# Idle ticks behind the last gather, matmuls with unread results at the start, and no marker copies in the last stage of a two-layer graph kernel

## The chip, the cores and the metric

The kernel runs on one core of a Trainium2 chip. A core has five engines that run side by side, each through its own list of instructions in order: TensorE (PE) multiplies matrices, VectorE (DVE) and GpSimd (POOL) do elementwise work and reductions, ScalarE (ACT) evaluates functions, and SyncE (SP) issues most of the transfers between the chip's memory and the core. GpSimd issues the indirect transfers, gathers and scatters by row number. Engines wait for each other through semaphores. The metric is the device time of one execution, in microseconds (us), as the median of several runs.

## The reference

There are 16 graphs of 1024 nodes with 128 features. Layer 0 is masked attention; layer 1 thins out each graph's edges and runs three graph convolutions with batch norms between them.

```python
h = max(layernorm(x), 0)
q, k, v = (relu(h @ W.T + b) for W, b in ((Wq, bq), (Wk, bk), (Wv, bv)))
att = softmax(where(adj, q @ k.T, -9e15))
x = x + relu((att @ v) @ Wo.T + bo)

h = max(layernorm(x), 0)
adj_d = dilate(adj)        # node after node: a node with more than 10 edges drops some of them
def sage(h, k):            # rows scaled to length 1
    out = (adj_d @ h / deg) @ Wr[k] + h @ Wx[k] + b[k]
    return out / norm(out)
h1 = bn(relu(sage(h, 1)));  h2 = bn(relu(sage(h1, 2)));  h3 = bn(relu(sage(h2, 3)))
x = x + concat(h1, h2, h3) @ Wl + bl
```

The batch norm takes mean and variance over all 16 graphs and all nodes, so no graph can enter a round before every graph has left the one before.

## The kernel before, in words

All of `fast` is one program written out by hand. Generators issue a few instructions and then yield; a loop decides which generator goes on when. Each engine then has its instructions in the order in which they were issued, and nothing is reordered later. `Clock` holds work that is put off: `later(n, fn)` (called `put_off` inside `Dilation`) runs `fn` in the n-th `tick()` from now.

**Start.** `load_x(0)` loads the features of graph 0, `load_adj(0)` (that is, `Dilation.load`) loads its adjacency matrix in eight blocks of 128 rows. Each block gets two instructions that run over 128x1024 elements: an exponential on ScalarE that writes the 0/1 matrix as bf16 and sums it (line 167), and a count of its zeros, which for graphs 0 and 1 is on VectorE (line 174). The buffer `st` of a block has three copies, so that a load waits for the exponential and the count of three blocks earlier. `project(0)` then makes layer norm on VectorE (`moments`, lines 564 to 583, and `normalize`, line 588), eight transposes on TensorE (line 598) and the projections to q, k and v (line 676). Two blocks of the matrix are processed ahead of `project(0)`, and 15 pieces of it are issued with one clock tick after each.

**Attention.** Sixteen steps of 48 ticks each, in which TensorE alternates between scores (line 697) and values (line 713), with the work of the dilation threaded between them by tables of ticks. For each pair of graphs the dilation sorts nodes, and `gather` (13 pieces) builds a one-hot matrix, turns it into row numbers (line 296), fetches 128 rows of the adjacency matrix by an indirect transfer on GpSimd (line 301), runs a scan over them on VectorE (line 305), makes codes (line 308), transposes them on TensorE (line 312), copies the result on ScalarE (line 316) and multiplies again (line 320). `solve` then iterates over a group of graphs. The gather of the last graph, 15, is not finished when attention ends: the plan puts its 13 pieces at ticks 68 to 94 of step 15, and only ticks up to 69 are run, so 11 pieces are left.

**Round one** of the convolutions (loop at line 1085) handles one graph per eight ticks. `mix` issues its matmuls and squares and norms, `turn` its transposes, `normalize` on GpSimd the layer norm of graphs further ahead. After each tick `beside1` (line 1073) advances `rest`, which is first what is left of the last gather and then `solve` for graphs 12 to 15 (118 pieces). How many pieces per tick is set by `PIECES1 / TICKS1`, 131 pieces in 120 ticks. Every fourth tick also moves the store of graph 15's layer 0 result, eight row scatters on GpSimd.

**Rounds two and three** are similar without the dilation. In round three the rows go back to their original order: graphs other than the five of `STAY` are scattered to a buffer `y_d` and loaded back, graphs of `STAY` are scattered straight to the output in the last stage. `pace_scatters` (line 1143) hands out one scatter in two of three ticks; ahead of each it issues on GpSimd a copy of one column into a tile `mark` that nothing reads (line 1149), out of the tile that VectorE wrote last, so that GpSimd waits for VectorE there.

**The last stage** (loop at line 1265) multiplies by the last third of `Wl` on TensorE (lines 1231 and 1239), adds on VectorE (line 1024), stores eleven graphs by SyncE (line 1247) and scatters the five of `STAY`, eight scatters of 128 rows each, on GpSimd (line 540). Then a flag is read, all engines meet at a barrier, and a general version would run if the flag said so.

Of the kernel before, what the change touches and what calls it, by code (L numbers as in the profile page):

```python
# [7 lines left out]
F32 = mybir.dt.float32  # L8
# [72 lines left out]
class Dilation:  # L81
# [76 lines left out]
    def load(self, b):  # L158

        nc = self.nc  # L160
        ab = self.rows.tile([P, NB, N], BF, name="ab", bufs=AB)
        diag = bass.AP(tensor=ab.tensor, offset=ab.offset, ap=[list(ab.ap[0]), [N + P, NB], [1, P]])
        self.A[b] = ab, diag
        for k in range(NB):
            st = self.rows.tile([P, N], F32, name="st", bufs=ST)
            nc.sync.dma_start(st, self.adj[b, k * P:(k + 1) * P, :])
            nc.scalar.activation(ab[:, k, :], st, AF.Exp, bias=self.one_k, scale=ONE_K,  # L167
                                 accum_out=self.deg[:, b, k:k + 1])
            yield
            junk = self.rows.tile([P, N], BF, name="junk", bufs=1)  # L170
            zeros = self.zeros[:, b, k:k + 1]
            if b < 2:

                nc.vector.scalar_tensor_tensor(junk, st, 0.0, self.onesf[:, 0:1].to_broadcast([P, N]),
                                               op0=OP.is_equal, op1=OP.mult, accum_out=zeros)
            else:
                nc.scalar.activation(junk, st, AF.Exp, scale=-ZERO_K, accum_out=zeros)  # L177
            yield

    def mirror(self, b, k):  # L180
# [332 lines left out]
def fast(ctx: ExitStack, tc: tile.TileContext, a, out, vp):  # L513
# [94 lines left out]
    def pieces(name, rows, pool):  # L608

        n = len(rows)  # L610
        v = pool.tile([3, 2, P], F32, name="pcv", bufs=1)[:, :n]
        part = pool.tile([3, 2, P], BF, name="pcp", bufs=1)[:, :n]
        acc = pool.tile([3, 2, P], F32, name="pca", bufs=1)[:, :n]
        res = pool.tile([3, n, 4, P], BF, name=name, bufs=1)
        for i, (base, more) in enumerate(rows):
            if base is None:
                nc.vector.tensor_copy(v[:, i, :], more)
            elif more is None:
                nc.vector.tensor_copy(v[:, i, :], base)
            else:  # L620
                nc.vector.tensor_add(v[:, i, :], base, more)
        for i in range(3):
            nc.vector.tensor_copy(part, v)
            if i == 0:
                nc.vector.tensor_scalar(acc, part, identf[:3, i:i + 1], None, op0=OP.mult)
            else:
                nc.vector.scalar_tensor_tensor(acc, part, identf[:3, i:i + 1], acc, op0=OP.mult, op1=OP.add)
            if i < 2:
                nc.vector.tensor_sub(v, v, part)
        nc.vector.tensor_copy(res, acc[:, :, None, :].to_broadcast([3, n, 4, P]))  # L630
        return [res[:, i].rearrange("p a b -> p (a b)") for i in range(n)]
# [9 lines left out]
    with ExitStack() as s1:  # L641
# [7 lines left out]
        def load_x(b):  # L649
            X[b] = xpool.tile([P, NB, XW], F32, name="xt")  # L650
            nc.sync.dma_start(X[b][:, :, :D], x_in[b].rearrange("(k p) d -> p k d", p=P))
            nc.vector.tensor_copy(X[b][:, :, D].bitcast(I32), dil.node32)

        def project(b):


            xt = X[b]
            hn = att.tile([P, NB, D], F32, name="hn", bufs=1)
            hT = att.tile([P, N], F32, name="hT", bufs=1)
            at = dict(name="pm", bufs=1) if b else dict(name="ps", bufs=2)  # L660
            ln = att.tile([P, 2, NB // 2, 2], F32, name="ln")
            engine = nc.gpsimd if b else nc.vector
            yield from moments(xt, att, ln[:, 0], ln[:, 1], engine)
            yield from normalize(engine, hn, xt, ln[:, 0], ln[:, 1])
            yield from transposed(hn, hT, lambda: aps, at["name"], at["bufs"])
            Q[b] = att.tile([P, N], F32, name="qT")
            K[b] = att.tile([P, N], F32, name="kT")
            vT = att.tile([P, N], F32, name="hn", bufs=1)
            V[b] = att.tile([P, NB, D + 1], F32, name="vw")
            nc.vector.memset(V[b][:, :, D], 1.0)  # L670
            for w, bias, o in ((wq, bq, Q[b]), (wk, bk, K[b]), (wv, bv, vT)):
                if o is vT:
                    at = dict(name="pm", bufs=1)
                for g in range(2):
                    pp = aps.tile([P, 512], F32, **at)
                    nc.tensor.matmul(pp, w, hT[:, 512 * g:512 * g + 512], start=True, stop=True)
                    later(1, lambda g=g, pp=pp, bias=bias, o=o: nc.scalar.activation(
                        o[:, 512 * g:512 * g + 512], pp, AF.Relu, bias=bias))
                    yield
            for g in range(2):  # L680
                pp = aps.tile([P, 4, P], F32, **at)
                for k in range(4):
                    j = 4 * g + k
                    nc.tensor.matmul(pp[:, k, :], vT[:, j * P:(j + 1) * P], wo, start=True, stop=True)
                later(1, lambda g=g, pp=pp: nc.vector.tensor_add(V[b][:, 4 * g:4 * g + 4, :D], pp,
                                                                 bo[:, None, :].to_broadcast([P, 4, P])))
                yield
# [67 lines left out]
        def solve_pieces(b0, b1):  # L755
            return 9 * ITER + 3 + 13 * (b1 - b0)
# [42 lines left out]
        bq, bk, bv = (column("L0_gnn_b" + n) for n in "qkv")  # L799
        bo = row_all("L0_gnn_bo")  # L800
        load_x(1)
        values0 = project(0)
        for _ in range(5 + 4 + 2 + 4):
            next(values0)
# [87 lines left out]
                    H[b] = enter(b)  # L892
                _advance(H[b][1])
        clock.flush()
        assert all(gen is gathering[B - 1] for gen, ticks in agenda if ticks)
        dil.tail = True
    load_x2(2)

    def last_of_dilation():

        yield from gathering[B - 1]
        yield from dil.solve(LAST, B)

    def last_stores():
# [158 lines left out]
    with tc.tile_pool(name="ps1", bufs=2, space=PSUM, reuse_waits="tile") as ps:  # L1063
        for _ in H[0][1]:
            clock.tick()
        rest, stores = last_of_dilation(), last_stores()
        checks = dil.verdict(a["nodemask"], vp, recips)
        _advance(checks)

        tick, TICKS1, PIECES1 = 0, 8 * (B - 1), 13 + solve_pieces(LAST, B)  # L1070
        entering = iter(())

        def beside1():
            nonlocal tick
            tick += 1
            _advance(rest, tick * PIECES1 // TICKS1 - (tick - 1) * PIECES1 // TICKS1)
            if tick % 4 == 0:
                _advance(stores)

            if tick in range(8 * LAST + 1, 8 * LAST + 15, 2) or tick > TICKS1:  # L1080
                _advance(checks)
            _advance(entering, tick * ENTER // 8 - (tick - 1) * ENTER // 8)

        prev = None
        for b in range(B):
            if b == B - 1:
                drain(rest)
            if b + 2 < B:
                H[b + 2] = enter(b + 2)
                entering = H[b + 2][1]  # L1090
            if b + 3 < B:
                load_x2(b + 3)
            ob = work.tile([P, NB, P], F32, name="ob")
            parts = {"mix": mix(b, H.pop(b)[0], wx[0], wr[0], bias0, None, ob, on_scalar=True)}
            if prev:
                parts["turn"] = turn(*prev)
            if b + 1 < B:
                parts["next"] = H[b + 1][1]
            in_turn(["mix", "mix", "next", "mix", "turn", "next", "mix", "turn"], parts, beside1)
            entering = iter(())  # L1100
            prev = (b, ob, r1[b // 2][:, b % 2, :])
        clock.flush()
        drain(turn(*prev))
        clock.flush()
        drain(checks)
# [5 lines left out]
    with big:  # L1111
# [26 lines left out]
        rows_r = lambda b: blocks(r2[b // 2][:, b % 2, :])  # L1138
        rows_z = lambda b: blocks(r1[b // 2][:, b % 2, :])
        mark = few.tile([P, 1], F32, name="mark")  # L1140
        waiting, ticks3 = [], 0

        def pace_scatters():


            nonlocal ticks3
            ticks3 += 1
            if ticks3 % 3 and waiting and waiting[0][0] <= ticks3:
                nc.gpsimd.tensor_copy(mark, last[0])  # L1149
                waiting.pop(0)[1]()  # L1150

        with tc.tile_pool(name="w3", bufs=3, reuse_waits="tile") as own:
# [109 lines left out]
        clock.flush()  # L1262
        (wl2,), pr = batchnorm(2, [wl[:, 2, :]])
        bias, = pieces("pc3", [(zrow, pr[:, 0, :])], few)
        for i, b in enumerate(order):
            parts = {"final": final(b, hs[b]), "raised": raise_next(i + 1)}
            in_turn(["raised", "final", "raised", "final"], parts, pace_scatters)
# [588 lines left out]
```

## Time and profile before

| | us |
|---|---|
| median of 3 runs | 1238.69 (1237.64 to 1240.6) |
| the profiled execution | 1234.29 |
| its span | 1232.4 |
| TensorE busy | 1095.0 (89%) |
| VectorE busy | 881.5 (72%) |
| ScalarE busy | 726.6 (59%) |
| GpSimd busy | 573.6 (47%) |

Stages in the span, by the first matmuls of each: attention from 14.4 us, round one from 787 us, round two from about 924 us, the last stage from about 1161 us. Times in what follows are microseconds from the start of the span. In a timeline line the first number is the start, the second the busy time of the merged group, then engine, line, operation, tiles (written, then read) and count; in brackets stands how long the engine sat idle before it, and what released it. In a line of waits stand the waiting instruction, what it waited for, the sum of waiting, the number of waits and the longest. A 128x512 matmul in f32 appears as two matrix passes.

### The profile page before, as it was taken

The page shows a single profiled execution, that of the slowest core. Times are in us where ns is not written, and L with a number is a line of the kernel's source. Part 1 is how long each engine was busy: PE and PEld are TensorE (multiplying, and loading weights), DVE is VectorE, ACT ScalarE, POOL GpSimd, SP SyncE. Part 2 cuts the span into 40 slices and gives each one's busy share as a digit, 9 for nine tenths or more (in the row PEclk, how much of TensorE's full clock was granted, in tenths as well). Part 3 has the DMA queues.
Part 4 walks back from the last instruction along what each step waited for, and adds up shares of the span by engine and source line. Part 5 has one row for each costly group of instructions (what it writes and reads, how often), then busy time and mean ns, then how long its engine had stood idle before and what let it go on. Part 6 is the DMA issues. An engine that isn't in the chain of part 4 may idle for free. (4 is left out here: it accounts for less than half of the span.)

```text
span 1232.4 us, 22348 instructions
## 1 busy us (share of the span) xinstructions
PE 1095.0 (89%) x7775; PEld 820.4 (67%) x7775; DVE 881.5 (72%) x2630; ACT 726.6 (59%) x1570; POOL 573.6 (47%) x1082
## 2 busy tenths in 40 slices
PE   4899999999899899899899888588769979999894
PEld 2467677666576676566567656477658758988773
DVE  5767567579788578678778778589877876666642
ACT  5578788777677777678677652266554542333320
POOL 0330752651742742743644524769400004777686
PEclk9899999999999999999999999789889989999897
DMA  6544244344244344244334411415000013778564
GB/s 197 157 132 139 92 139 152 99 130 150 87 137 144 98 137 153 86 126 151 97 127 122 125 31 39 122 42 135 1 1 1 1 35 109 228 218 239 167 185 126
DMA packets 118147, 143.45 MB, mean 116 GB/s; under 512 B 9212, under 2 KB 94088, under 8 KB 118024
## 3 DMA queue, kind: packets, MB, share of 16 engines
q1 hardware_dynamic: 106120, 110.78, 30.3%
q0 software_dynamic: 11904, 31.15, 7.7%
q8 instruction: 63, 1.03, 0.4%
q14 instruction: 60, 0.49, 0.1%
HBM read 113.39 MB, written 28.51 MB: 115 GB/s over the span
## 5 line engine op out<-in xcount | busy, mean ns | idle before, releaser
L713 PEld LDWEIGHTS po<-vw,e 128*128 128x128 f32 x2048 | 273.1, 195 | 65.7 <-issue 65.3
L713 PE MATMUL po<-vw,e 128*128 128x129 f32 x2048 | 306.9, 284 | 0.0
L697 PE MATMUL ps<-qT,kT 128*128 128x512 f32 x512 | 272.0, 615 | 0.8 <-ACT e L699 0.8
L700 DVE TENSOR_TENSOR e<-e,ab 128x512 f32<-128x512 f32 x256 | 177.9, 696 | 110.4 <-ACT e L699 108.8
L699 ACT ACTIVATE e<-ps 128x512 f32<-128x512 f32 x256 | 153.0, 598 | 107.1 <-PE ps L697 84.4
L540 POOL DMA_INDIRECT x_d<-xt,slot x128 | 142.6, 1114 | 38.8 <-issue 34.9
L167 ACT ACTIVATE ab<-st,d_one_k 128x1024 bf16<-128x1024 f32 x128 | 146.9, 1148 | 0.3 <-DMA st<-in_adj_dram 0.3
L576 POOL TENSOR_SCALAR ln_t<-ln_st 128x8 f32<-128x8 f32 x31 | 8.0, 258 | 288.5 <-DVE ln_st L569 230.0
L177 ACT ACTIVATE junk<-st 128x1024 bf16<-128x1024 f32 x112 | 118.3, 1056 | 0.0
L540 POOL DMA_INDIRECT y_d<-y,nodes x88 | 86.2, 979 | 29.1 <-issue 28.6
L722 ACT ACTIVATE o<-po,recips 128x128 f32<-128x128 f32 x128 | 46.7, 367 | 72.1 <-DVE recips L720 72.0
L697 PEld LDWEIGHTS ps<-qT,kT 128*128 128x128 f32 x512 | 79.0, 194 | 7.6 <-issue 3.1
L1019 ACT ACTIVATE r<-pt 128x512 f32<-128x512 f32 x74 | 44.5, 601 | 58.7 <-PE pt L1007 58.7
L588 POOL TENSOR_SCALAR hn<-xt,ln 128x128 f32<-128x128 f32 x120 | 75.9, 644 | 1.6
L965 ACT ACTIVATE sq<-po 128x512 f32<-128x512 f32 x80 | 47.7, 596 | 47.1 <-PE po L956 44.1
L951 PE MATMUL po<-ws,r 128*128 128x128 f32 x512 | 74.8, 292 | 0.0
L305 DVE TENSOR_TENSOR_SCAN left<-rows 128x1024 f16<-128x1024 f32 x16 | 38.2, 2389 | 50.1 <-DMA rows<-in_adj_dram,row 50.1
L1016 DVE BATCH_NORM_STATS2 stats<-r 128x6 f32<-128x512 f32 x74 | 50.9, 689 | 29.4 <-ACT r L1019 28.9
L951 PEld LDWEIGHTS po<-ws,r 128*128 128x128 f32 x512 | 64.9, 199 | 8.6 <-issue 6.8
L968 DVE TENSOR_REDUCE nrm<-sq 128x4 f32<-128x512 f32 x80 | 53.9, 676 | 22.8 <-ACT sq L965 21.4
L1149 POOL COPY mark<-y 128x1 f32<-128x1 f32 x30 | 5.7, 191 | 135.7 <-DVE y L1024 132.8
L588 POOL TENSOR_SCALAR hn<-xt 128x128 f32<-128x128 f32 x112 | 55.9, 510 | 27.0 <-PE pt L598 26.2
(300 smaller groups left out, 2426.8 us busy)
## 6 DMA issues: line engine op xcount, KB each, us to landing
st<-in_adj_dram SPq DMA_DIRECT2D x128, 512.0 KB, 3.7
r<-y_d SPq DMA_DIRECT2D x22, 512.0 KB, 5.2
xt<-x_d SPq DMA_DIRECT2D x16, 524.0 KB, 3.8
xt<-in_x_dram SPq DMA_DIRECT2D x16, 512.0 KB, 4.2
x<-x_d SPq DMA_DIRECT2D x16, 512.0 KB, 4.4
out_dram<-r SPq DMA_DIRECT2D x11, 512.0 KB, 3.4
x_d<-xt,slot POOLq DMA_INDIRECT x128, 2.8
y_d<-y,nodes POOLq DMA_INDIRECT x88, 3.5
```

Of the source, the lines that this page charges most:

```text
L167: nc.scalar.activation(ab[:, k, :], st, AF.Exp, bias=self.one_k, scale=ONE_K, accum_out=self.deg[:, b, k:k + 1])
L177: nc.scalar.activation(junk, st, AF.Exp, scale=-ZERO_K, accum_out=zeros)
L540: d = nc.gpsimd.indirect_dma_start(out=dst, out_offset=bass.IndirectOffsetOnAxis(ap=slots, axis=0), in_=src, in_offset=None)
L588: engine.tensor_scalar(hn[:, k, :], xt[:, k, :D], minus[:, k // 2, k % 2, None], rstd[:, k // 2, k % 2, None], op0=OP.add, op1=OP.mult)
L697: nc.tensor.matmul(p, K[b][:, k * P:(k + 1) * P], Q[b][:, c], start=True, stop=True)
L699: later(1, lambda: nc.scalar.activation(e, p, AF.Exp))
L700: later(2, lambda: nc.vector.tensor_mul(e, e, AB_[b][:, k, c]))
L713: nc.tensor.matmul(po[:, q % 2, :], E[k][:, i * P:(i + 1) * P], V[b][:, k, :], start=(k == 0), stop=(k == NB - 1))
L951: nc.tensor.matmul(po[:, i, :], hT[:, c:c + P], wxk, start=(i == 3), stop=False)
L965: later(1, lambda: nc.scalar.activation(sq, halves[g], AF.Square))
L968: nc.vector.tensor_reduce(n[:, 0, 4 * g:4 * g + 4], sq, axis=AX.X, op=OP.add)
L1016: nc.vector.bn_stats(stats[:, 2 * b + g, :], d)
```

## The change

Four edits. In `load`, the zero count becomes a function; for graph 0's first two blocks it is put off by eight ticks, which places both counts behind six of the eight `normalize` instructions of `project(0)`. Ahead of `project(0)` GpSimd fills a 128x512 tile with ones and TensorE multiplies it six times with the identity matrix into a PSUM tile that is next written by the v projection; nothing reads the six results. In round one, after the gather's piece 5 (the indirect transfer) six ticks go by without a piece of `rest`, after piece 7 (the codes) five; `PIECES1` becomes 11 + 11 + 118 = 140 for the same 120 ticks. From the third batch norm on, `pace_scatters` issues no copy into `mark`.

```diff
@@ load
-            junk = self.rows.tile([P, N], BF, name="junk", bufs=1)
+            junk = lambda: self.rows.tile([P, N], BF, name="junk", bufs=1)
             zeros = self.zeros[:, b, k:k + 1]
-            if b < 2:
-
-                nc.vector.scalar_tensor_tensor(junk, st, 0.0, self.onesf[:, 0:1].to_broadcast([P, N]),
+
+            def count(st=st, zeros=zeros):
+                nc.vector.scalar_tensor_tensor(junk(), st, 0.0, self.onesf[:, 0:1].to_broadcast([P, N]),
                                                op0=OP.is_equal, op1=OP.mult, accum_out=zeros)
+
+            if b == 0 and k < 2:
+
+                self.put_off(8, count)
+            elif b < 2:
+
+                count()
             else:
-                nc.scalar.activation(junk, st, AF.Exp, scale=-ZERO_K, accum_out=zeros)
+                nc.scalar.activation(junk(), st, AF.Exp, scale=-ZERO_K, accum_out=zeros)
@@ fast, ahead of project(0)
         load_x(1)
+
+        some = att.tile([P, 4 * P], F32, name="e", bufs=16)
+        nc.gpsimd.memset(some, 1.0)
+        idle = aps.tile([P, 4 * P], F32, name="pm", bufs=1)
+        for _ in range(6):
+            nc.tensor.matmul(idle, identf, some, start=True, stop=True)
         values0 = project(0)
@@ fast, between attention and round one
-        assert all(gen is gathering[B - 1] for gen, ticks in agenda if ticks)
+        (gather_left,) = (len(ticks) for gen, ticks in agenda if ticks)
...
+    GATHER_IDLE = {5: 6, 7: 5}
+
     def last_of_dilation():
 
-        yield from gathering[B - 1]
+        for part in range(13 - gather_left, 13):
+            next(gathering[B - 1])
+            for _ in range(1 + GATHER_IDLE.get(part, 0)):
+                yield
         yield from dil.solve(LAST, B)
@@ round one
-        tick, TICKS1, PIECES1 = 0, 8 * (B - 1), 13 + solve_pieces(LAST, B)
+        tick, TICKS1, PIECES1 = 0, 8 * (B - 1), gather_left + sum(GATHER_IDLE.values()) + solve_pieces(LAST, B)
@@ pace_scatters
-        waiting, ticks3 = [], 0
+        waiting, ticks3, marked = [], 0, True
...
-                nc.gpsimd.tensor_copy(mark, last[0])
+                if marked:
+                    nc.gpsimd.tensor_copy(mark, last[0])
@@ last stage, after the third batch norm
         bias, = pieces("pc3", [(zrow, pr[:, 0, :])], few)
+        marked = False
         for i, b in enumerate(order):
```

On VectorE the new order in round one puts, between the row numbers and the scan of the last gather, the reduction, the maximum, the reciprocal and the two scalings of graph 0 (lines 968, 990, 994, 997). On TensorE it puts all of graph 1's matmuls and the four transposes of each half of graph 0's result (line 1007) ahead of the codes' transposes (line 312). On ScalarE the two copies of line 316 come behind the square root of graph 1 (line 991). GpSimd's order changes only by the new memset and the 40 copies that are gone.

## The prediction

> **What bounds the kernel.** The chain that ended last is short here (only the final scatters), so I read each of the three places where the change acts in the timelines and waits, and the stretches around them in busy time by window. TensorE is busiest (89%), so what counts is where it waits.
>
> Start, timeline of VectorE and TensorE:
>
> ```profile
> 7.03 1.23 DVE L174 SCALAR_TENSOR_TENSOR junk<-st,d_onesf 128x1024 bf16<-128x1024 f32 x1 [3.87 <-DMA st<-in_adj_dram]
> ...
> 9.62 1.40 DVE L569 BATCH_NORM_STATS2 ln_st<-xt 128x6 f32<-128x256 f32 x4
> ...
> 13.97 2.14 DVE L588 TENSOR_SCALAR hn<-xt,ln 128x128 f32<-128x128 f32 x8
> ...
> 16.43 3.65 PE L676 MATMUL ps<-hT,w_L_gnn_Wq 128*128 128x512 f32 x4
> 19.87 2.11 PE L676 MATMUL ps<-hT,w_L_gnn_Wk 128*128 128x512 f32 x4
> ```
>
> VectorE idles 3.87 us for the matrix, counts twice (7.03 to 9.62), and only then starts the layer norm on which everything else waits. Four passes took 3.65 us for q and 2.11 for k: TensorE was slow until about 20 us.
>
> Round one, waits from 785 to 835, then VectorE's and GpSimd's timeline:
>
> ```profile
> PE pb L312 <- DVE codes L308: 12.1, 1, 12.1
> DVE left L305 <- DMA rows<-in_adj_dram,row: 8.7, 1, 8.7
> ```
>
> ```profile
> 789.93 0.16 DVE L299 TENSOR_SCALAR row<-pb 128x1 int32<-128x1 f32 x1 [1.87 <-PE pb L296]
> ...
> 799.12 3.80 DVE L305 TENSOR_TENSOR_SCAN left<-rows 128x1024 f16<-128x1024 f32 x1 [8.70 <-DMA rows<-in_adj_dram,row]
> 802.95 1.28 DVE L308 SCALAR_TENSOR_TENSOR codes<-rows,left 128x1024 f16<-128x1024 f32 x1
> 804.16 0.67 DVE L968 TENSOR_REDUCE nrm<-sq 128x4 f32<-128x512 f32 x1
> ...
> 794.01 1.07 POOL L301 DMA_INDIRECT rows<-in_adj_dram,row  x1 [0.16 <-issue]
> ```
>
> The row numbers are ready at 790.1, GpSimd gets to the gather at 794.01 (it is in its scatters before), the rows land at 799.12. VectorE stands at the scan, TensorE at the codes' transposes, and graph 1, which needs neither, is queued behind both.
>
> The end, GpSimd's timeline, and SyncE's waits from 1217 on:
>
> ```profile
> 1163.08 0.96 POOL L540 DMA_INDIRECT y_d<-y,nodes  x1 [0.30 <-issue]
> 1164.34 0.96 POOL L540 DMA_INDIRECT y_d<-y,nodes  x1 [0.30 <-issue]
> ...
> 1220.79 0.98 POOL L540 DMA_INDIRECT out_dram<-r,nodes  x1 [0.16 <-issue]
> 1221.78 0.20 POOL L1149 COPY mark<-r 128x1 f32<-128x1 f32 x1
> 1222.14 0.98 POOL L540 DMA_INDIRECT out_dram<-r,nodes  x1 [0.16 <-issue]
> ...
> SPq L508 <- SPq L508: 3.4, 1, 3.4
> SPq L507 <- DMA out_dram<-r,nodes: 1.7, 2, 1.3
> ```
>
> Scatters follow each other every 1.36 us with a copy (1169.04 to 1222.14 in 39 steps) and every 1.265 without (1159.28 to 1166.87 in six). SyncE waits 3.4 us for its own last store, and then 1.3 us for GpSimd at the barrier.
>
> [...] 3.65 against 2.11 us, and half the clock in the stretch 44 to 46 us after a gap with little work. [...] the scan took 3.80 us beside GpSimd's layer norm here and 2.31 at 774.42. [...] where the trace has 5.1 from issue to scan.
>
> **Part 1, counts put off.** The counts' 2.59 us stay ahead of the last two normalizations, so the second half of the layer norm gains only what VectorE can start before 7.03. The 1,024 packets of x's rows (those under 2 KB) had gone by about 5.0 us; the first matrix block's by about 5.9, and it was seen at 7.03. The same lag of 1.1 puts x at 6.1: gain 0.9 us, between 0 (x at 7.03) and 1.8. The buffers freed later, at about 13 and 14.4 us instead of 10.4, cost nothing while the transfers ahead of them (1.5 MB, until about 15.7 us) fill the DMA engines; without that cover a block would be 2.6 us late.
>
> **Part 2, six matmuls.** Twelve passes, from the identity and the memset (about 2.3 us[...]) on, cost 11 us if all slow (3.65/4 each) and 6.3 at the fast 2.11/4, and end by 8.6 to 13.3; the first transposes can come at 6.1 + 4.35 + 0.3 = 10.8. So up to 2.5 us of delay for the first transposes, which the second half, due at 15, hides. A fast clock saves 1.54 us on q (3.65 - 2.11). But the transposes that VectorE feeds singly and the 2.6 us of counts leave TensorE nearly idle from about 10 to 15, enough to fall back. I take 0.7 of 0 to 1.9. Behind this, ScalarE is busy without gap from 22.6 to 31 us on what q and k release, and SyncE's later loads wait for it, so the shift travels. Start: 1.6 us.
>
> **Part 3, idle ticks.** GpSimd's order is unchanged, so the rows still land at 799.1, codes are still done at about 804.2. What moves into the gap is graph 0's norm: before, reduction to second scaling ran from 804.16 to 809.10, 4.94 us with 2.21 of waiting for ScalarE (a table load). Now it runs from 792.9 (squares done) to about 796, and VectorE still waits some 3 us for the rows. After 804.2 VectorE does graph 1's norm while ScalarE and TensorE turn the codes, and reaches line 323 at about 809.4 as before (809.57), one graph further. TensorE: graph 1's matmuls start at 792.3, wait about 1.5 us for GpSimd's normalized rows, end near 799.8, then 4.4 us of wait: 5.9 for 12.05, so 6.1 gained. The rest of the round is then 13 graphs beside the same 118 pieces, at 9.3 instead of 8.7 pieces per graph. A graph's period is 6.0 to 6.8 us (line 927 at 812.95, 818.99, 825.69, 832.47), but from 840 to 880 VectorE is busy 35.8 of 40 us and TensorE 33.9, so I count VectorE's gain: 5 us, between 2 and 6.7. Late next: the scan itself, then solve for graphs 12 to 15, now ending at tick 120 and not 118; graph 15's mix needs it at about 125.
>
> **Part 4, no copies.** 40 scatters at 0.096 less are 3.8 us, and the first needn't wait for VectorE's second addition (0.9 more): GpSimd ends 4.7 us sooner, at 1218.4. VectorE's additions keep ahead of it (graph 14's at 1205.8 and 1207.6, its scatters from about 1208.6). Then SyncE's last store is late: issued at 1217.45 behind a TensorE without gaps since 1161, and landed at 1222.0 to 1222.6. Only the 1.3 us at the barrier and a little for a freer DMA are won: 1.5, between 0.8 and 3.
>
> **Sum.** 1.6 + 5 + 1.5 = 8.1 us. The profiled execution took 1234.29 (span 1232.4, 1.9 around it) and would take 1226.2; the median of the runs lies 4.4 above it, so 1238.7 - 8.1 = 1230.6, rounded to 1230.5.
>
> **Rivals.** *More than that:* TensorE's reckoning holds (6.7), the clock stays fast (2.8 at the start), the store lands sooner (3): 12.5 us, 1226 and below. For it: TensorE's 12.05 us of wait. Against: VectorE's load in round one. *The gap is given back:* the new places of solve's pieces cost part of it, gather 2 or less, 5 in all or less: 1234 to 1236. For it: TensorE already waits for solve's masks (0.43 per graph, once 1.28). *No change:* the attention stage swallows the start, round one is set by solve, and only the tail's 1 to 2 us stay: 1236.2 to 1239. Against: nothing in the trace has a fixed date. *Slower:* solve's denser pieces make TensorE wait in every graph; the waits at its line 413 are 3.51 and 2.08 us before. It decides from 8.1/13 = 0.62 us more per graph on; at 1 us more, 13 - 8 = 5 slower, 1244. Against: the same pieces in total, and two idle ticks between a mask and its matmul as before.
>
> **Numbers.** Forecast (1226.5 to 1234) 0.62; more 0.14; given back 0.12; no change 0.07; slower 0.05. What can be told from no change is 0.2%, 2.5 us: faster (below 1236.2) 0.88, within 0.07, slower 0.05. Range 1223.5 to 1236.5: it cuts the last two cases and the end of the second.
>
> **What would show it.** Layer norm statistics at about 6.1 and q's four passes nearer 2 than 3.65 us; graph 1's line 927 (now 946) at about 792 and the wait at the codes' transposes at 4 to 5 us; copies gone and scatters 1.265 apart, with SyncE no longer waiting for GpSimd at the barrier. The prediction is wrong if round one's graphs take over 7.4 us each, if the rows land later than before, or if the end follows GpSimd's last scatter by its full 4.7 us.

## The result, and the profile after

The changed kernel takes 1231.16 us (median of 5 runs, 1228.0 to 1232.8); the kernel before, beside it, 1240.08 (1237.64 to 1240.6). The ratio is 0.9926, with a 95% interval from 0.9908 to 0.9944: 0.74% faster, 8.9 us. The forecast was 1230.5, or 8.2 us below the 1238.69 from which it was reckoned.

The two profiled executions differ by far less, 1234.29 against 1232.79 us, so they can't be subtracted as wholes. Cut into stages they can be read (start: up to ScalarE's first score exponential; attention: from there to the first matmul that writes `ph` from `wr` and `hT`; round one: from there to the first batch-norm aggregate; end: from the third such aggregate to the end of the span):

| us | start | attention | round one | round two | round three | end |
|---|---|---|---|---|---|---|
| before | 24.87 | 762.29 | 133.49 | 91.10 | 145.68 | 74.97 |
| after | 23.56 | 766.81 | 131.80 | 91.76 | 145.46 | 71.51 |

Attention, whose code is the same in both, took 4.5 us more in the profiled execution after. In ten profiles from quick chips, on which the kernel before takes 1236 to 1240 us, it runs from 762.3 to 769.8 us, and the one of before is the lowest of all. The stages that the change touches are each shorter.

**Start.** VectorE's timeline after:

```profile
5.17 1.41 DVE L576 BATCH_NORM_STATS2 ln_st<-xt 128x6 f32<-128x256 f32 x4 [1.54 <-DMA xt<-in_x_dram]
...
11.07 1.22 DVE L174 SCALAR_TENSOR_TENSOR junk<-st,d_onesf 128x1024 bf16<-128x1024 f32 x1
...
13.49 0.60 DVE L595 TENSOR_SCALAR hn<-xt,ln 128x128 f32<-128x128 f32 x2
```

The statistics no longer wait for the matrix and its counts; they start when x lands, at 5.17 instead of 9.62. The counts now stand ahead of the last two normalizations, which end at 14.09 (before: 13.97 + 2.14 = 16.11). TensorE's timeline after:

```profile
1.98 7.45 PE L814 MATMUL pm<-e,identf 128*128 128x512 f32 x12 [1.98 <-POOL e L811]
...
13.88 0.73 PE L605 MATMUL ps<-identf,hn 128*128 128x128 f32 x2 [2.34 <-DVE hn L595]
14.41 3.62 PE L683 MATMUL ps<-hT,w_L_gnn_Wq 128*128 128x512 f32 x4
17.82 2.85 PE L683 MATMUL ps<-hT,w_L_gnn_Wk 128*128 128x512 f32 x4
```

The unread matmuls ran in 7.45 us and were out of the way by 9.43, but q still took 3.62 us, as before (3.65), and k even 2.85 (2.11). The granted clock shows a part of it. Each line below has a stretch and its length, the busy time and count of TensorE, its weight loads, VectorE, ScalarE and GpSimd, the mean granted share of TensorE's clock, and the DMA's share and GB/s:

```profile
6.11:12.93 6.82, 4.93 (x14) 1.97 (x12) 6.27 (x26) 4.25 (x6) 0.00 (x0) 1.00 0.70 206
12.93:19.76 6.83, 5.88 (x9) 2.57 (x10) 3.34 (x9) 1.97 (x3) 0.00 (x0) 0.50 0.78 266
```

The matmuls did get quicker, 4.45 us for the first five passes and 3.00 for the other seven, but at 12.93, ahead of q, the granted clock fell to half, and it stayed there until 19.76. It isn't all that sets q's time: in the profile before it reads 1.00 from 16.4 to 20.0, where q took 3.65 us.

**Round one.** Waits from 788 to 838 (waiting instruction, what it waited for, sum, number, longest):

```profile
PE pb L319 <- DVE codes L315: 5.7, 1, 5.7
...
DVE left L312 <- DMA rows<-in_adj_dram,row: 3.3, 1, 3.3
```

VectorE's and GpSimd's timeline:

```profile
802.54 4.56 DVE L312 TENSOR_TENSOR_SCAN left<-rows 128x1024 f16<-128x1024 f32 x1 [3.33 <-DMA rows<-in_adj_dram,row]
807.13 1.27 DVE L315 SCALAR_TENSOR_TENSOR codes<-rows,left 128x1024 f16<-128x1024 f32 x1
...
797.20 1.07 POOL L308 DMA_INDIRECT rows<-in_adj_dram,row  x1 [0.16 <-DVE nrm L1009]
...
801.13 3.46 POOL L595 TENSOR_SCALAR hn<-xt 128x128 f32<-128x128 f32 x8
```

TensorE's wait for the codes is 5.7 us where it was 12.1, VectorE's for the rows 3.3 where it was 8.7. The rows land 12.2 us into the stage, as before (12.0). But the scan, which doesn't belong to the change, took 4.56 us for 3.80.

What TensorE gains up to the third graph isn't all kept. Round one in stretches as above, cut at the first matmul of line 927 (946) of the third graph; before:

```profile
787.16:812.95 25.79, 13.74 (x101) 11.76 (x101) 12.23 (x28) 9.82 (x33) 16.51 (x27) 0.74 0.40 115
812.95:920.65 107.70, 87.32 (x675) 73.00 (x673) 91.44 (x262) 62.76 (x231) 59.23 (x128) 0.94 0.17 46
```

and after:

```profile
790.37:809.29 18.92, 11.79 (x92) 9.72 (x93) 10.75 (x18) 9.31 (x31) 16.71 (x27) 0.88 0.54 154
809.29:922.17 112.88, 89.43 (x683) 75.06 (x681) 95.00 (x272) 63.77 (x232) 58.88 (x127) 0.94 0.16 44
```

The third graph starts 6.9 us sooner, and TensorE's idle time up to there is 7.1 us for 12.1. In the rest of the round it is 23.5 us for 20.4. A part of this comes with work that moved there (the end of the gather, some pieces of `solve`); TensorE's waits for results of `solve` alone are 16.9 us for 12.5.

**End.** GpSimd's timeline, and SyncE's waits from 1215 on:

```profile
1218.31 0.96 POOL L547 DMA_INDIRECT out_dram<-r,nodes  x1 [0.30 <-issue]
1219.58 0.96 POOL L547 DMA_INDIRECT out_dram<-r,nodes  x1 [0.30 <-issue]
```

```profile
SPq L1873 <- PEq L1873: 3.4, 2, 2.8
SPq L515 <- SPq L515: 3.3, 1, 3.3
```

The scatters follow each other every 1.265 us without a copy between them, and SyncE no longer waits for GpSimd ahead of the barrier. At the barrier itself it still stands 2.8 us. In the same view of before, this was its longest wait:

```profile
SPq L1852 <- PEq L1852: 5.1, 2, 4.6
```

Both times GpSimd is the last to arrive there, as its closing steps show further down. The stretch from the third aggregate on is 3.5 us shorter.

### The profile page after: what moved, and what is told of

It reads as the page before. It is cut to its first block, busy times and chain, and to the rows that moved or that the text cites. A ratio compares the mean times of both kernels' runs of the same rounds, so it can differ in the third digit from the quotient of the medians.

```text
span 1230.9 us, 22315 instructions
## 1 busy us (share of the span) xinstructions
PE 1106.3 (90%) x7787; PEld 824.2 (67%) x7787; DVE 883.8 (72%) x2630; ACT 728.2 (59%) x1570; POOL 567.2 (46%) x1043
## 4 chain that ended last, share of the span: by engine, by line
PE 56%; DVE 23%; ACT 6%; POOL 6%; issue 4%; DMA 4%; POOLq 0%; DVEq 0%; ACTq 0%; SPq 0%
PE ps L704 10%; PE po L720 10%; PE po L970 6%; PE pm L683 6%; DVE e L707 4%; DMA rows<-in_adj_dram,row 4%; PE pt L1026 3%; PE ph L1194 2%; PE ph L1251 2%; DVE left L312 2%; PE ph L1195 2%; POOL hn L595 2%; PE po L975 2%; ACT e L706 2%; DVE m L369 2%
## 5 line engine op out<-in xcount | busy, mean ns | idle before, releaser
L987 DVE TENSOR_REDUCE nrm<-sq 128x4 f32<-128x512 f32 x80 | 53.9, 676 | 24.6 <-ACT sq L984 23.3
L199 DVE SCALAR_TENSOR_TENSOR junkv<-pd,ab 128x64 bf16<-128x64 int32 (+7 forms) x128 | 57.8, 451 | 15.1 <-PE pd L193 15.1
```

The costliest lines, as they stand in the source:

```text
L199: nc.vector.scalar_tensor_tensor(junk.rearrange("p a b -> p (a b)")[:, :n], pt.rearrange("p a b -> p (a b)").bitcast(I32)[:, :n], 1.0, ab[ ...
```

## The experiments

The kernels ran in three sets, each beside the kernel before on the same chip.

### Each part alone

Each kernel is the one before with one hunk of the change: the counts put off; the six matmuls; the idle ticks with the new pace; the copies left out.

```diff
@@ e1_counts, load
+            if b == 0 and k < 2:
+                self.put_off(8, count)
@@ e2_matmuls, ahead of project(0)
+        for _ in range(6):
+            nc.tensor.matmul(idle, identf, some, start=True, stop=True)
@@ e3_idle, ahead of round one
+    GATHER_IDLE = {5: 6, 7: 5}
@@ e4_marks, last stage
+        marked = False
```

> Only the two zero counts of graph 0 put off by eight ticks; nothing else changed. By the prediction's part 1 the first projections come about 0.9 us earlier (up to 1.8) and the shift travels: 0.5 to 2 us faster in the median. The rival, that the attention stage swallows whatever the start gains, expects a first score exponential at 23.5 us instead of 24.9 and a time that cannot be told from before.

> Only the six matmuls with unread results. By part 2 they give 0 to 1.5 us: q's four passes (3.65 us before) come down towards 2.1 only if TensorE's clock is still fast when the projections start. In this kernel VectorE's layer norm begins at 9.6 us as before, so TensorE is idle from about 9.4 to 14.4 and I expect q at 3.6 us and no gain; the rival expects q near 2.1 us and 1.5 us gained.

> Only the eleven idle ticks behind the last gather and the new pace of 140 pieces in 120 ticks. By part 3 round one (from its first matmul to its batch norm's aggregation, 133.5 us in the profile before) gets 5 us shorter, and the whole 2 to 6.7 faster. The rival, that the denser solve pieces give much of it back, expects 131 to 132 us for round one as in the profile of the changed kernel, and about 2 us in all.

> Only the copies in the last stage left out. By part 4 the last store of SyncE takes over as the end, and 1.5 us are gained (0.8 to 3). The rival, which the profile of the changed kernel suggests, is that the end follows GpSimd's last scatter because GpSimd's own closing steps are the last thing to run: then 3.5 to 4.7 us are gained, and from the third aggregation to the end of the span it takes 70.3 to 71.5 us instead of 75.0.

The kernel before took 1235.96 us here.

| part alone | median, us | ratio to before, 95% interval | its stage in the profile, us |
|---|---|---|---|
| counts put off | 1234.56 | 0.9983 (0.9964 to 1.0002) | start 23.16 |
| six matmuls | 1236.92 | 0.9999 (0.9981 to 1.0016) | start 23.78 |
| idle ticks | 1234.48 | 0.9988 (0.9969 to 1.0008) | round one 127.87 |
| no copies | 1233.64 | 0.9983 (0.9967 to 0.9999) | end 71.76 |

Single runs of one kernel lie up to 9 us from its median (before: 1230.39 to 1245.11 over 75 runs), so only the copies' part stands clear of 1, and barely. The four together make 0.47% with an uncertainty of about 0.4; the whole change had 0.74. That the parts help each other isn't shown. The profiles say more than the times, since in one stage only one part is at work, though each is a single execution:

- start without part 1 and 2: 24.87, 23.57 and 24.11, mean 24.2; with the counts alone 23.16; with the matmuls alone 23.78 and no shorter q (3.12 us, where kernels with neither have 3.10 to 3.65);
- end with a copy: 74.97, 74.51, 76.21, 75.77; without: 71.76 and 71.51.

### The changed kernel again, without the matmuls, with warmer ones, and with two copies

```diff
@@ f2_parts134, ahead of project(0)
-        for _ in range(6):
-            nc.tensor.matmul(idle, identf, some, start=True, stop=True)
@@ f3_warm, in the loop that issues the 15 pieces of project(0)
+            if n == 5 + 4:
+                for _ in range(2):
+                    nc.tensor.matmul(idle, identf, some, start=True, stop=True)
@@ f4_two_copies, pace_scatters
-                if marked:
+                for _ in range(1 if marked else 2):
                     nc.gpsimd.tensor_copy(mark, last[0])
```

In f3_warm piece 9, counted from 0, is the first half of the transposes; the two matmuls come on top of the six. f1_changed is the changed kernel itself.

> The changed kernel itself again, beside the others of this call. If the parts add up, its gain is near the sum of the four measured alone (1.4 - 1.0 + 1.5 + 2.3 = 4.2 us by their medians); if they help each other, or the first runs flattered it, it is nearer the 8.9 us measured at first. In its profile the stretch from the last batch-norm aggregate to the end should again be 71.5 us, and round one (first matrix product of round one to the first batch-norm aggregate) tells how far the 131.8 us seen before is the rule: 128 as in the kernel with the idle ticks alone, if nothing but the place of GpSimd's work differs from execution to execution.

> All of the change but the six matmuls. Theory: the matmuls' warmth is lost before q, so leaving them out costs nothing; q stays 3.6 us, k falls back from 2.85 to 2.1 to 2.4, the first score exponential comes about 0.4 us earlier than in the changed kernel, and the time is within 1 us of it. Rival: the matmuls are worth 0.7 us as predicted, and the time is that much above the changed kernel's.

> The changed kernel with two more unread matmuls between the two halves of the first transposes, where TensorE idled 2.34 us. Theory: TensorE's clock falls back in this idle stretch and in the sparse transposes ahead of it; filled, q takes 2.1 to 2.5 us instead of 3.6 and the first score exponential comes 1.0 to 1.5 us earlier. Rival: what makes q slow is not the idle stretch (the transposes alone are too sparse for the fast clock); then q stays at 3.6 us, and the added matmuls, 4 slow passes, delay the second half by up to 1 us.

> The changed kernel with two copies of the mark ahead of each scatter of the last stage, where the change has none and the kernel before has one. Theory: the end follows GpSimd's last scatter, because its closing steps come after it; with some 0.2 us more for each of 40 scatters and a start behind VectorE's addition, the stretch from the last batch-norm aggregate to the end is about 79 us (75.4 with one copy, 71.6 with none), the time 7 us above the changed kernel's. Rival, as predicted: SyncE's last store sets most of the end, and GpSimd only what lies beyond it; then from one copy to none only 1.5 us are won, and from two to one all of the added time, so 5.5 us above the changed kernel's.

This set ran on another chip, on which the kernel before takes 1280.63 us.

| us | median | ratio, 95% interval | start | round one | end |
|---|---|---|---|---|---|
| f1_changed | 1275.79 | 0.9970 (0.9944 to 0.9995) | 23.05 | 129.47 | 93.83 |
| f2_parts134 | 1274.95 | 0.9954 (0.9934 to 0.9974) | 22.43 | 131.83 | 90.61 |
| f3_warm | 1273.99 | 0.9953 (0.9934 to 0.9972) | 21.36 | 127.85 | 91.18 |
| f4_two_copies | 1274.02 | 0.9945 (0.9926 to 0.9964) | 22.26 | 131.42 | 89.47 |

Two results are clear. Leaving out the six matmuls costs nothing that can be seen. And two more of them between the halves of the transposes, together with the six, do what the six were to do; TensorE's timeline of f3_warm, and a stretch of it:

```profile
11.59 1.45 PE L820 MATMUL pm<-e,identf 128*128 128x512 f32 x3
...
14.60 1.98 PE L683 MATMUL ps<-hT,w_L_gnn_Wq 128*128 128x512 f32 x4
16.41 2.07 PE L683 MATMUL ps<-hT,w_L_gnn_Wk 128*128 128x512 f32 x4
```

```profile
12.93:19.76 6.83, 5.91 (x16) 2.08 (x15) 3.19 (x9) 3.90 (x6) 0.00 (x0) 1.00 0.80 275
```

q takes 1.98 us for 3.62, and the first exponential comes 1.7 us earlier than in f1_changed. The clock, which fell to half at 12.93 in the profile after, is full here throughout. Whether the two would do without the six wasn't tried. In the profile after, TensorE was busy for 1.61 of the 3.50 us from the end of the six (9.43) to the fall at 12.93, with six single small transposes fed by VectorE, and the longest wait, 2.34 us, ended only at 13.88. In this profile so much work did not hold the clock; where the bound lies isn't shown.

The third result contradicts the expectation: with two copies per scatter the end took 1.1 to 4.4 us less than in the three kernels without any, not 7 more (the times can't be told apart). On this chip the last stage goes another way. VectorE's timeline of f1_changed around the turn from one graph of `STAY` to the next (every third graph of the last stage), and GpSimd's:

```profile
1230.08 1.28 DVE L1043 TENSOR_TENSOR r<-r,ph 128x512 f32<-128x512 f32 x2 [3.66 <-remote]
...
1227.45 0.95 POOL L547 DMA_INDIRECT out_dram<-r,nodes  x1 [0.31 <-issue]
1231.64 0.96 POOL L547 DMA_INDIRECT out_dram<-r,nodes  x1 [3.24 <-DVE r L1043]
```

By the profile, in which the ends of matmuls are modelled, TensorE was done with what the addition reads at 1227.95 (the bias matmul of line 1259, 0.38 us from 1227.57), yet the addition starts at 1230.08, 1.7 us after GpSimd's last scatter of the graph before has ended (1228.40), and GpSimd then waits 3.24 us for the addition. This repeats from each graph of `STAY` to the next, 1.6 to 1.7 us after the last scatter each time (2.1 the first time), and TensorE waits behind it (2.28 us, until 1230.82). With two copies GpSimd is so far behind that it isn't waiting, and VectorE's later additions follow TensorE. On the chip of the other two sets the same program shows none of this. What holds the addition isn't settled: the instruction waits for TensorE alone by its semaphores, and the profile names no engine ("remote"). ScalarE's copy of line 1242, which waits for TensorE too, starts at 1230.20 with the same mark, which points to a late signal from TensorE and not to a slow VectorE.

The very end is another one here as well; f1_changed in the list of events (each line with its count, shortest, median and longest time in ns, and the first and last start):

```profile
L1873 POOLq DRAIN  x3: 40/103/4979, 1260.4 to 1272.5; - x3
...
L515 SPq EVENT_SEMAPHORE  x8: 17/17/17, 1269.8 to 1270.3; - x8
```

GpSimd has finished its long closing step at 1265.40 and then stands until 1272.03: SyncE's last store, issued at 1265.34, sets the end. The same holds in f2_parts134 and f3_warm. In f4_two_copies GpSimd is last again (1273.26). So copies can cost little here. The kernel before was not profiled on this chip, so what part 4 does there in full stays open.

### The changed kernel once more, warm, with the copies, and with more idle ticks

```diff
@@ g3_with_copies, last stage
-        marked = False
@@ g4_more_idle, ahead of round one
-    GATHER_IDLE = {5: 6, 7: 5}
+    GATHER_IDLE = {5: 10, 7: 7}
```

g2_warm has the edit of f3_warm.

> The changed kernel once more, beside the next three. In the last call, on a chip where the kernel before took 1280.6 us [...], it won 0.3%; on the first chip 0.7%. On a chip as quick as the first, theory: 0.9926 of the time before again, with the stretch from the last batch-norm aggregate to the end at 71.5 us. On one like the last: 0.997 again, and that stretch above 90 us, since there VectorE's first addition of each third graph came only 1.7 us after GpSimd's last scatter of the graph before it.

> Two more unread matmuls between the halves of the first transposes, as in the last call, where q took 1.98 instead of 3.62 us and the first score exponential came at 21.36 instead of 23.05 us. Theory: the same again on any chip, and the time 1 to 1.7 us below the changed kernel's. Rival: the attention stage swallows the earlier start, and the time is the same.

> The changed kernel without part 4: one copy of the mark ahead of each scatter of the last stage, as before the change. Theory: on a quick chip the end follows GpSimd, and the stretch from the last batch-norm aggregate to the end is 75 to 76 us again, 3.6 to 4.5 more than without copies, in the time too. Rival from the last call: where VectorE's additions wait for GpSimd, the copies cost nothing, since GpSimd waits for those additions anyway; then the times are equal or this one is up to 3 us lower, with a stretch of about 85 to 90 us.

> Idle ticks 10 and 7 in the place of 6 and 5 behind the last gather: solve starts later still and its pieces are 9.6 per graph. Theory: what is left of the wait for the rows (VectorE 3.3 us, TensorE 5.7 us) is filled with graph 1's norm, so the wait at the codes' transposes falls below 3 us; but the denser solve beside GpSimd takes it back, and round one stays at 128 to 132 us, the time within 1 us of the changed kernel's. Rival: the gap is what counts, round one falls by another 2 to 3 us, and the time with it.

This set ran on the chip of the first one; the kernel before took 1238.35 us.

| us | median | ratio, 95% interval | start | round one | end |
|---|---|---|---|---|---|
| g1_changed | 1226.79 | 0.9913 (0.9880 to 0.9946) | 22.54 | 127.20 | 71.56 |
| g2_warm | 1227.95 | 0.9904 (0.9872 to 0.9937) | 21.13 | 133.00 | 72.29 |
| g3_with_copies | 1232.24 | 0.9951 (0.9937 to 0.9966) | 23.08 | 128.85 | 74.32 |
| g4_more_idle | 1227.95 | 0.9919 (0.9889 to 0.9950) | 22.82 | 126.83 | 72.34 |

**The copies** are worth 0.38% here, some 4.7 us, though the two intervals just overlap, and 2.8 us in the stretch of the profile. Where they go is seen in what GpSimd does after its last scatter. By the list of events, before:

```profile
L508 POOLq INC_SWDGE_SEM  x1: 1395/1395/1395, 1225.2 to 1225.2; - x1
...
L1852 POOLq DRAIN  x3: 40/103/4979, 1226.6 to 1232.1; - x3
```

and after:

```profile
L515 POOLq INC_SWDGE_SEM  x1: 1395/1395/1395, 1223.7 to 1223.7; - x1
...
L1873 POOLq DRAIN  x3: 40/103/4979, 1225.1 to 1230.6; - x3
```

Before, the last scatter ends at 1223.12; GpSimd waits until 1225.15 for the rows to land, signs off its transfers (1.40 us) and drains from 1226.58 (4.98 us); 0.84 us later the span ends. All of this is fixed behind the last landing: 1.40 + 4.98 + 0.84 = 7.2 us, and neither SyncE nor anyone else has to be waited for meanwhile. After the change the last scatter ends at 1220.54, but its landing is waited for until 1223.66: 3.1 us and not 2.0 (g1_changed 3.4, g3_with_copies 2.0). So of what GpSimd gains at its scatters it loses 1.1 to 1.6 at the landing, by the five profiles without copies from quick chips. SyncE's last store is now issued at 1220.89, right behind the last scatter, where it was issued at 1217.45 and had four scatters still behind it. While the landing was waited for, the DMA engines were 11% busy before (34 GB/s, 1223.12 to 1225.20) and 73% after (219 GB/s, 1220.89 to 1224.00); that the store delays the landing is the likely cause, and wasn't tried by itself.

**More idle ticks** fill the gap for good: TensorE's wait at the codes' transposes is down to 0.72 us. Round one gains 0.4 us and the time nothing: TensorE idles 0.5 us up to the third graph where it was 3.7 in g1_changed, but 26.3 in the rest of the round where it was 23.0. So what is left of the gap isn't worth filling in this way.

**Why round one differs from one profile to the next** is seen in VectorE's and GpSimd's timeline of g1_changed:

```profile
799.36 2.29 DVE L312 TENSOR_TENSOR_SCAN left<-rows 128x1024 f16<-128x1024 f32 x1 [2.19 <-DMA rows<-in_adj_dram,row]
...
798.10 6.48 POOL L595 TENSOR_SCALAR hn<-xt 128x128 f32<-128x128 f32 x8
...
804.78 0.87 POOL L595 TENSOR_SCALAR hn<-xt 128x128 f32<-128x128 f32 x2
```

In the profile after, the scan took 4.56 us and GpSimd's eight normalizations 3.46, and the line for its next two is

```profile
804.79 3.94 POOL L595 TENSOR_SCALAR hn<-xt 128x128 f32<-128x128 f32 x2
```

So GpSimd loses the same 3.0 us in both, at the eight or at the two. In all fourteen profiles the scan ends together, within 0.3 us, with one of GpSimd's small instructions, which takes 2.2 to 2.5 us in the place of 0.44 or less. From the start of that instruction to the scan's end pass 2.2 to 2.4 us; what varies is the time from the scan's start until it began, from nothing to 2.25 us. The kernel's 15 other scans took 2.28 to 2.36 us in the profile before and 2.28 to 2.32 in the one after. That the scan and the small instruction hold each other up is the author's reading; no run tests it by itself. What decides when the scan gets on stays open.

TensorE waits behind the scan for the codes (5.74 us in the profile after, 3.33 in g1_changed). Its only wait for GpSimd's normalizations from 786 to 812 is 1.28 us at 798.82 (0.30 in g1_changed), ahead of the scan. With the idle ticks, a scan of 2.29 to 2.31 us goes with a round one of 127.2 and 127.9 us, one of 4.08 to 4.56 with 128.9, 131.8 and 133.0. The last two also show a second loss of some 1.5 us at the eighth graph (a period of 7.2 and 7.3 us for 5.7): the granted clock was 0.76 and 0.77 in this period, and 1.00 in g1_changed.

**Warm** starts 1.4 us earlier again, with q at 1.98 us. Its ratio is below the changed kernel's in both sets, by 0.17% and 0.09%, both differences lie within the intervals, and in the second set its median is the higher one: an improvement at its place that the time doesn't resolve.

## Why the prediction was right

The time was forecast within 0.7 us, but the terms were not all of the forecast size. From the profiles of the quick chips, the mean of kernels without a part against those with it:

| | without, us | with, us | gain | forecast |
|---|---|---|---|---|
| start, parts 1 and 2 | 24.2 (3 profiles) | 23.0 (4) | 1.2 | 1.6 |
| round one, part 3 | 132.9 (4) | 129.7 (5) | 3.1 | 5, from 2 to 6.7 |
| end, part 4 | 75.2 (5) | 71.9 (5) | 3.3 | 1.5, from 0.8 to 3 |
| sum | | | 7.6 | 8.1 |

A part too high and a part too low made up for each other. That the sum fits so closely is luck.

**Part 1**, "The same lag of 1.1 puts x at 6.1: gain 0.9 us": x was there at 5.17, the whole of the bound of 1.8, and the normalizations end 1.3 to 2.0 us earlier; at the first exponential 1.0 us of it is left (24.2 to 23.16, where the kernels without the part vary from 23.57 to 24.87). The size came out right, but by luck: x came 0.9 us sooner than assumed, and about as much was lost again on the way to the exponential.

**Part 2**, "I take 0.7 of 0 to 1.9": it is nothing that can be seen. The failing step is the weight given to "A fast clock saves 1.54 us on q"; the sentence after it, that the stretch from about 10 to 15 us is idle enough for the clock to fall back, is what happened (half the clock from 12.93), and f3_warm shows that the 1.54 (here 1.64) is there once two more matmuls stand in this stretch.

**Part 3**: the mechanism at the gap was right: of TensorE's 12.05 us of wait 1.5 for GpSimd's rows and 4.4 at the codes were to be left, and 1.28 and 5.74 were (0.30 and 3.33 in g1_changed); VectorE's "some 3 us" for the rows were 3.33, and graph 1's line came 4.9 us into the stage, as forecast. Two steps failed. The first is "codes are still done at about 804.2": it took the scan's 3.80 us over unchanged, and with the idle ticks the scan takes 2.29 to 4.56 us on the quick chips. The second is the rest of the round, where TensorE's 6.1 was lowered to VectorE's 5 and nothing was put down for longer waits for `solve`. TensorE in round one, as the means of the same nine profiles:

| us | without part 3 | with | |
|---|---|---|---|
| idle up to the third graph | 11.8 | 5.5 | 6.3 less |
| idle from there on | 21.2 | 23.3 | 2.1 more |
| busy | 99.9 | 101.0 | 1.1 more |

Up to the third graph TensorE's reckoning (6.1) came true. Of this, 2.1 us are given back behind it, with 16.5 to 16.9 us of waiting for `solve` in all nine profiles with these idle ticks, the slow chip's included, and 12.5 to 13.7 in those without. So the rival that `solve`'s new places give the gap back holds in part. TensorE's busy time varies from 98.4 us (g3_with_copies, granted clock 0.97 from the third graph on) to 103.3 (g2_warm, 0.92), so that the last 1.1 us need not belong to the change. VectorE's reckoning of 5 is met only where the scan is quick, by 132.9 - 127.2 = 5.7 in g1_changed and 5.0 in e3_idle, and some 1 us of these belongs to the scan, which took 3.31 to 3.80 in the kernels without. By its own sign, graphs of over 7.4 us, the prediction would have been wrong: from the third graph to the last they take 7.6 to 7.9 us each. The sign was badly set, since the kernels without the part take 7.3 to 7.4; the 6.0 to 6.8 behind it were read from four early graphs.

**Part 4** was mis-sized: "Then SyncE's last store is late ... Only the 1.3 us at the barrier and a little for a freer DMA are won: 1.5". SyncE's store does land later than GpSimd's last rows (1225.2 against 1223.7), but SyncE's closing steps are short and end at 1227.4, whereas GpSimd's sign-off and drain, 6.4 us, come behind its last landing and end at 1230.1. On the quick chips the end follows GpSimd's last landing; on the slow one, without copies, it followed SyncE's store after all. Neither 1.3 nor the full 4.7 is right: 4.5 less at the last scatter (65.7 to 61.1 us after the aggregate), minus 1.1 to 1.6 for the later landing. The forecast showed SyncE's waits without the longest of them, 4.6 us at the barrier, and never asked what GpSimd still had to do once it had issued its last transfer.

## What to carry to other kernels

Ask of every engine that issues transfers what it must do after the last one: here GpSimd's 1.40 and 4.98 us stood behind its last landing, while SyncE, done 2.2 us after its own, could land 1.5 us later without harm. Ask too where work that is to keep TensorE quick lies: here six matmuls that ended 4.98 us ahead of q left q at 3.62 us, and two more among the transposes went with 1.98 us at a granted clock of 1.00. Where a gap is filled, count what the moved work costs later: here a third of the gain in the gap was given back. The scan beside GpSimd's row of small instructions took 2.29 us in one profile of the changed kernel and 4.56 in another, so one profile isn't enough to size an edit there, and the stage that nobody touched may vary more than the edit is worth (attention by 7.5 us, the whole change by 8.9).

## What the runs showed that was not expected

- The attention stage, with the same code, took 762 to 770 us from one profile to the next on the quick chips, nearly as much as the whole gain of the change.
- On one chip the kernel before took 3.4% longer (1280.63 against 1238.35 us). Attention took 787 to 794 us there and the end 89 to 94. By an estimate from the mean granted clocks these account for a part only: 0.951 over the 1272.8 us of f1_changed is 62 us of clock lost, 0.961 over the 1230.9 of the profile after is 48. The rest is not explained.
- On that chip, at the turn from one graph of `STAY` to the next, VectorE's addition came 1.6 to 1.7 us after GpSimd's last scatter, with its input ready 0.7 to 2.1 us before by the modelled ends of the matmuls, and two copies between the scatters did no harm. A gain in such a place can depend on the chip.
- GpSimd's sign-off and drain after indirect transfers take 1.395 and 4.979 us, the same to the ns in all fourteen profiles.
- 512 KB of rows by an indirect gather, 1.07 us of issue included, took 5.1 to 5.6 us to the scan's start.
